# Three empty turns before a node cell's rows, and the first chunk of each unit of layer 3 freed from waiting for the gathering

## The chip, the cores and the metric

The kernel runs on one core of one Trainium2 chip. The metric is device time in microseconds (us) of one execution. A core has a matrix engine (TensorE, in the profile PE, with its weight loads as PEld), a vector engine (VectorE, DVE), an activation engine (ScalarE, ACT), a general engine (GpSimd, POOL) and SyncE (SP), which here only issues transfers (DMAs). Each engine works off its own instructions in a fixed order and waits where an operand isn't ready. Sums of matmuls arise in PSUM, a small memory of eight banks; everything else lies in SBUF or in the chip's main memory.

## What is computed

Four graph layers run over the same 2708 nodes with 256 features and one dense 2708 x 2708 matrix `adj` (non-negative, with a full diagonal). After each layer the input is added and the rows are normalised.

```python
x = _layernorm(x + _L0_gnn_ref(x, adj, ...))   # adj @ (x * W)
x = _layernorm(x + _L1_gnn_ref(x, adj, ...))   # attention with 4 heads
x = _layernorm(x + _L2_gnn_ref(x, adj, adj, ...))
x = _layernorm(x + _L3_gnn_ref(x, adj, ...))
# layer 2, for adj without negative entries
node_support = adj_without_diagonal @ h
edge_output = gru_cell(node_support, h, edge weights)
edge_support = mean over 3 heads of softmax(e_plus where adj > 0) * adj @ (h @ W)
node_output = gru_cell(edge_support, h, node weights)
layer 2 = diag(adj) * edge_output + diag(adj) * node_output
# layer 3
z = concat([x, adj @ (x @ neigh_W.T) / (adj.sum(1) + 1)]) @ lin_W.T
```

## The kernel before

The change touches layers 2 and 3. Both are long products with `adj`, whose columns are cut into three **units** and whose rows into eleven **chunks** of 256. A unit of layer 2 takes 512, 512 and 330 columns from each half of the nodes and goes three times (heads) through the eleven chunks. A unit of layer 3 takes 430, 430 and 366 columns from each half and goes through them once; the last two full tiles of layer 3 are done in another way at the end.

**One chunk** is a call of `seven` (line 299). It makes one step of a fast 2 x 2 block product that needs seven products in place of eight. First DVE forms four sums of the four blocks in `pa` (lines 305 to 308), two of them in a tile `s` that has two buffers. Then PE makes seven products, which the profile shows as fourteen matmuls of line 318. Three of the seven use a block as it was loaded (a11, a12, a22); the other four use a sum. All add up in seven PSUM banks, named m1, m26, m75 and m43. In layer 2, ACT and DVE first make the block from the attention logits (lines 1288, 1291, 1292); in layer 3 the block comes straight from `adj` by SP's transfers (line 265). `pa` has three buffers.

**Gathering.** At the end of a head, or of a unit in layer 3, `gathered` (line 322) reads the seven banks back: a copy by ACT (line 326) and four DVE instructions in the order of lines 329, 332, 335 and 336. The next chunk's products into m26, m75 and m43 have to wait for the reads of these. The last of the four is kept as `summed`.

**Work between the products.** The eighth PSUM bank (`bank`, line 1074, one buffer) serves everything else: projections of a head's result (`project`, line 1115), the gates of the two GRU cells (`cell`, line 1132), the transposes and products of the finished rows (`node_rows` and `rows_end`, lines 1173 and 1184), and layer 3's rows (`rows3`, line 1340). These are Python generators. `between` (line 292) advances the first of them to its next `yield`: this is one **turn**. `urgent` (projections) goes ahead of `later`. `seven` gives a turn after its third and its sixth product, so a chunk has two turns; in the first seven chunks of layer 3's first unit (`early3`, line 1358) there is one after each product. Work that is left is run off without products between, before the first chunk that needs the last rows (line 1361).

`node(u, est)` (line 1226) does the node cell of unit u for its two halves. For one half, `cell` takes eight turns, one for each gate. After the last gate, DVE still has the lines 1165, 1166, 1246 and 1247 to do before the result `yt` is there; this runs in a turn of its own, in which PE gets nothing. Then, in turns of their own, each tile of up to 128 rows is turned (`node_rows`: line 1178, ACT's copy at 1180, moments by DVE and POOL at 171 to 176) and ended (`rows_end`: the product of line 1189, which ACT reads at 1191 and DVE at 1192; then POOL stores the row). The order of turns is rows 0, rows 1, end 0, rows 2, end 1, and so on. Where a tile of rows straddles two units, POOL first copies its part (line 1219). During the first half's rows, the second half's inputs are loaded through POOL's queue (line 1247, issue at line 247), and DVE later mixes them (`prepare`, lines 1240 and 1241).

**Who orders the work.** The program is traced in Python order. The framework then plans each engine's order before the run, by simulated readiness: of the instructions that it takes to be ready, the one that was traced first goes first. An instruction may so stand before one that was traced earlier but is ready later. On the chip this order is fixed. `tc.issue_after(x)` tells the planner to put every instruction of the block that runs on x's engine behind x in that order. In layer 3 it holds the four sums of every chunk behind `summed`, the end of the gathering before:

```python
for i, c in enumerate(lead):
    ...
    with tc.issue_after(summed.ins):
        seven(nright, m, pa, h3, hq[c], c, w, i == 0, i == MH - 1, range(7) if early3 else (2, 5))
y, summed = gathered(nleft, m, w, W, "yk")
```

Of the kernel before, what the change touches and what calls it, by code (L numbers as in the profile page):

```python
# [2 lines left out]

# [24 lines left out]
def kernel(  # L28
# [59 lines left out]
    def sz(i):  # L88
        return min(P, N - i * P)
# [189 lines left out]
    def quarter_sums(pool, b, c, nm):  # L279

        tt = pool.tile([P, 4, P], F32, tag=f"quarter{c}", name=f"{nm}{c}")
        b11, b12 = b[2 * c][:, :P], b[2 * c][:, P:]
        b21, b22 = b[2 * c + 1][:, :P], b[2 * c + 1][:, P:]
        nc.vector.tensor_tensor(tt[:, 0], b12, b11, ALU.subtract)
        nc.vector.tensor_tensor(tt[:, 1], b22, tt[:, 0], ALU.subtract)
        nc.vector.tensor_tensor(tt[:, 2], b12, b22, ALU.subtract)
        nc.vector.tensor_tensor(tt[:, 3], b21, tt[:, 1], ALU.subtract)
        return tt
# [3 lines left out]
    def between():  # L292
        for q in (urgent, later):
            while q:
                if next(q[0], q) is not q:
                    return
                q.pop(0)
# [24 lines left out]
    def gathered(pool, m, w, wide, tag, bufs=1):  # L322

        m1, m26, m75, m43 = m
        m1s = pool.tile([P, wide], F32, tag="m1s", name="m1s", bufs=1)
        nc.scalar.copy(m1s[:, :w], m1[:, :w])
        y = pool.tile([P, FC, 2, wide], F32, tag=tag, name=tag, bufs=bufs)
        yq = y.rearrange("p f h w -> p (f h) w")[:, :, :w]
        nc.vector.tensor_tensor(
            yq[:, 0::3], m1s[:, None, :w].to_broadcast([P, 2, w]), m26[:, :, :w], ALU.add  # L330
        )
        nc.vector.tensor_tensor(
            yq[:, 1:3], yq[:, 3:4].to_broadcast([P, 2, w]), m75[:, :, :w], ALU.add
        )
        nc.vector.tensor_tensor(yq[:, 3], yq[:, 1], m75[:, 1, :w], ALU.add)  # L335
        return y, nc.vector.tensor_tensor(yq[:, 1:3], yq[:, 1:3], m43[:, :, :w], ALU.add)
# [726 lines left out]
    with (  # L1063
# [7 lines left out]
        summed = None  # L1071
# [30 lines left out]
        def accumulators():  # L1102
            return [ps_a.tile([P, W], F32, tag="m1", name="m1")] + [
                ps_a.tile([P, 2, W], F32, tag=nm, name=nm) for nm in ("m26", "m75", "m43")
            ]
# [67 lines left out]
        def node_rows(t, src):  # L1173

            n = sz(t)
            pt = bank()
            for f in range(FC):
                nc.tensor.transpose(pt[:n, f * P : (f + 1) * P], src[:, f, :n], ident)
            y = nleft.tile([P, F], F32, tag="y", name="y", bufs=3)
            nc.scalar.copy(y[:n], pt[:n, :F])  # L1180
            mean, rs = moments(y, n)
            return t, src, y, mean, rs

        def rows_end(t, src, y, mean, rs):

            n = sz(t)
            pz = bank()
            for f in range(FC):
                nc.tensor.matmul(pz[:n], src[:, f, :n], lwn[:, f, :], start=(f == 0), stop=(f == FC - 1))
            nc.vector.tensor_scalar(y[:n], y[:n], mean, rs, ALU.subtract, ALU.mult)  # L1190
            nc.scalar.activation(h3[t][:n], pz[:n, F:], AF.Copy, scale=rs)
            nc.vector.scalar_tensor_tensor(y[:n], pz[:n, :F], rs, y[:n], ALU.mult, ALU.add)
            nc.gpsimd.dma_start(y3_d[t], y[:n])

        def load_cell(lo, w):
            got = []
            for parts, tag in ((xt_d, "xt2"), (edge_d.values(), "et")):
                got.append(nleft.tile([P, FC, W], F32, tag=tag, name=tag))
                load_columns(got[-1], parts, lo, w, nc.gpsimd)
            return got  # L1200

        def load_diag(lo, w):

            dst = nleft.tile([P, W], F32, tag="drow", name="drow")
            src = bass.AP(tensor=diag_d.tensor, offset=diag_d.offset + lo, ap=[[0, P], [1, w]])
            nc.gpsimd.dma_start(dst[:, :w], src)
            return dst

        def by_tiles(lo, w, src, ends, among=range(NT)):

            tiles, at = [], 0
            for t, c0, c1 in pieces(lo, w, among):
                got = src(at, c1 - c0)
                at += c1 - c0
                if c1 - c0 < sz(t):
                    first = t not in ends
                    if first:
                        ends[t] = nleft.tile([P, FC, P], F32, tag=f"yt{len(ends)}", name=f"yt{t}")
                    nc.gpsimd.tensor_copy(ends[t][:, :, c0:c1], got)
                    if first:  # L1220
                        continue
                    got = ends[t]
                tiles.append((t, got))
            return tiles

        def node(u, est):

            a, w = units[u]
            nxt = None
            for h in range(2):  # L1230
                lo = h * NH + a
                xt, et = nxt or load_cell(lo, w)
                drow = load_diag(lo, w)
                yt = nleft.tile([P, FC, W], F32, tag="yt", name="yt")
                parts = [[a[:, j, :w] for j in range(FC)] for a in (xt, et, yt)]

                def prepare(j):

                    xj, ej, _ = (a[j] for a in parts)
                    nc.vector.tensor_tensor(ej, ej, drow[:, :w], ALU.mult)  # L1240
                    nc.vector.tensor_tensor(ej, ej, xj, ALU.add)

                def rest(j):

                    _, ej, yj = (a[j] for a in parts)
                    nc.vector.tensor_tensor(yj, yj, drow[:, :w], ALU.mult)
                    nc.vector.tensor_tensor(yj, yj, ej, ALU.add)

                yield from cell(est[h], xt, yt, w, *node_w, b_node, prepare, rest)
                yield  # L1250
                tiles = by_tiles(lo, w, lambda at, n: yt[:, :, at : at + n], shared)
                got = []
                for i in range(len(tiles) + 1):
                    if i < len(tiles):
                        got.append(node_rows(*tiles[i]))
                        yield
                    if i:
                        rows_end(*got[i - 1])
                        yield
                    if i == 1 and h == 0:  # L1260
                        nxt = load_cell(NH + a, w)
# [15 lines left out]
        for u, (_, w) in enumerate(units):  # L1277
            est = [nleft.tile([P, FC, W], F32, tag="est", name="est", bufs=3) for h in range(2)]
            for k in range(K):
# [23 lines left out]
                y, summed = gathered(nleft, m, w, W, "yk")  # L1303
# [6 lines left out]
        def complete(u):  # L1310

            return [t for t in tiles3 if ends3[t] == u]
# [27 lines left out]
        def rows3(u, y, o8):  # L1340

            a, w = units3[u]
            for h in range(2):
                for t, src in by_tiles(h * NH3 + a, w, lambda at, n: y[:, :, h, at : at + n], shared3, tiles3):
                    pt = room()
                    for f in range(FC):
                        nc.tensor.transpose(pt[: sz(t), f * P : (f + 1) * P], src[:, f, : sz(t)], ident)
                    row3(t, o8[:, complete(u).index(t)], pt)
                    yield
            flush()  # L1350
# [4 lines left out]
        for u, (_, w) in enumerate(units3):  # L1355
            m = accumulators()
            for i, c in enumerate(lead):
                early3 = u == 0 and max(ends_at[2 * c], ends_at[2 * c + 1]) + 1 < len(units)
                if u == 0:
                    if not early3:  # L1360
                        while urgent or later:
                            between()
                    hq[c] = quarter_sums(xqp, h3, c, "hq")
                pa = nright.tile([P, 2, 2, W], F32, tag="p", name="p", bufs=3)
                load_pairs(units3, u, c, pa, NH3, tiles3)
                if i == MH - 3:
                    o8 = hold.tile([P, 4 * W // F, F], F32, tag="blk", name="o8", bufs=2)
                    for j, t in enumerate(complete(u)):
                        nc.gpsimd.dma_start(o8[: sz(t), j], y3_d[t])
                with tc.issue_after(summed.ins):  # L1370
                    seven(nright, m, pa, h3, hq[c], c, w, i == 0, i == MH - 1, range(7) if early3 else (2, 5))
            y, summed = gathered(nleft, m, w, W, "yk")
            later.append(rows3(u, y, o8))
# [287 lines left out]
```

## Time and profile before

| what | value |
|---|---|
| runs before, median (lowest to highest) | 1877.79 us (1877.62 to 1879.04), 3 runs |
| the profiled execution's own time | 1876.67 us |
| its span, first to last instruction | 1874.9 us |
| mean granted clock of TensorE | 0.998 of full speed |
| PE busy | 1833.9 us, 98% of the span |
| DVE busy | 1295.4 us, 69% |
| ACT busy | 691.6 us, 37% |
| POOL busy | 262.0 us, 14% |
| layer 2's heads | first gathering ends at 997.3 us, last at 1625.8 us |
| layer 3's gatherings | lines 329 to 336 at 1730.9, 1788.6 and 1840.2 us |

The span is the time from the first to the last instruction. A row of the timeline gives the start, the length, the engine, the line, the operation, what it writes and reads, how many instructions are merged in it, and in brackets how long the engine was idle before it and what ended that. The list of waits sums such idle times by line and by what ended them. A small letter q after an engine marks its sequencer, which issues transfers. Times of POOL are rough, and a matmul's end is modelled.

### The profile page before, as it was taken

What the parts mean: (1) busy time and instruction counts of PE and PEld (TensorE: products, weight loads), DVE (VectorE), ACT (ScalarE), POOL (GpSimd) and SP (SyncE); (2) the same over time, 40 slices, a digit from 0 to 9 for tenths busy, and PEclk for the clock granted to TensorE, in tenths of its full rate; (3) what the DMA queues carried; (4) which work ended last, traced back from release to release, by engine and by line L of the source; (5) the groups of instructions that cost most, each with busy time, mean ns of one, the idle gap of its engine ahead of it and who ended that gap; (6) DMA issues with size and microseconds to landing.
All of it is one profiled execution on the core that took longest, in us unless ns stands there. A gap on an engine that the chain in (4) does not pass through costs nothing. (4 is left out here: it accounts for less than half of the span.)

```text
span 1874.9 us, 23105 instructions
## 1 busy us (share of the span) xinstructions
PE 1833.9 (98%) x7530; PEld 1033.8 (55%) x7530; DVE 1295.4 (69%) x2302; ACT 691.6 (37%) x1420; POOL 262.0 (14%) x427
## 2 busy tenths in 40 slices
PE   8999999999999999999999999999999999999997
PEld 7788842232345887888444444444445555654555
DVE  5334479999897664754558887777887768855664
ACT  4445410033143203111556665555564555321011
POOL 1211120001012411000002000111100302111111
PEclk9999999999999999999999999999999999999999
DMA  8344410000002667754556665454554535634763
GB/s 296 124 155 146 152 48 1 30 1 11 13 7 69 144 145 186 180 133 114 175 142 204 180 177 155 126 161 124 155 154 110 141 102 132 163 105 116 199 167 117
DMA packets 434653, 237.32 MB, mean 127 GB/s; under 512 B 184299, under 2 KB 421516, under 8 KB 432092
## 3 DMA queue, kind: packets, MB, share of 16 engines
q1 hardware_dynamic: 417438, 207.41, 40.4%
q0 software_dynamic: 8208, 22.59, 3.8%
q10 hardware_dynamic: 8878, 5.76, 1.0%
q8 instruction: 62, 1.02, 0.2%
q14 instruction: 67, 0.55, 0.1%
HBM read 223.00 MB, written 12.66 MB: 126 GB/s over the span
## 5 line engine op out<-in xcount | busy, mean ns | idle before, releaser
L793 DVE SCALAR_TENSOR_TENSOR p<-fall_b,rise,mask 128x1024 f32<-128x1024 f32 (+1 forms) x264 | 293.9, 1157 | 32.5 <-PE den L784 16.7
L1288 ACT ACTIVATE p<-st,e_neg 128x1024 f32<-128x1024 f32 (+1 forms) x198 | 197.3, 1040 | 197.0 <-PE m L318 193.3
L318 PE MATMUL m<-s,xq 128*128 128x512 f32 (+3 forms) x660 | 230.3, 467 | 0.0
L775 PE MATMUL acc<-p,h 128*64 128x512 f32 (+2 forms) x1056 | 214.5, 548 | 0.2 <-ACT sum L806 0.2
L318 PE MATMUL m<-p,xq 128*128 128x512 f32 (+1 forms) x396 | 183.0, 544 | 0.1
L212 PE MATMUL acc<-turn,strip 128*128 128x257 f32 x792 | 181.6, 379 | 0.0
L1291 ACT ACTIVATE p<-p 128x1024 f32<-128x1024 f32 (+1 forms) x198 | 178.7, 942 | 0.2
L305 DVE TENSOR_TENSOR s<-p 128x512 f32<-128x512 f32 (+3 forms) x132 | 81.7, 619 | 125.1 <-PE m L318 96.2
L318 PE MATMUL m<-p,x 128*128 128x512 f32 (+1 forms) x396 | 167.7, 542 | 0.3 <-DVE supt L335 0.3
L318 PEld LDWEIGHTS m<-s,xq 128*128 128x128 f32 x660 | 124.5, 190 | 76.3 <-issue 59.0
L1292 DVE TENSOR_TENSOR p<-p,blk 128x1024 f32<-128x1024 f32 (+1 forms) x132 | 143.0, 1103 | 32.6 <-ACT p L1291 21.9
L212 PEld LDWEIGHTS acc<-turn,strip 128*128 128x128 f32 x792 | 147.3, 190 | 20.3
L775 PEld LDWEIGHTS acc<-p,h 128*64 128x64 f32 x1056 | 69.8, 136 | 138.2 <-issue 128.6
L318 PE MATMUL m<-s,x 128*128 128x512 f32 (+3 forms) x330 | 127.2, 467 | 0.0
L784 PE MATMUL den<-p,h 128*32 128x512 f32 (+2 forms) x1056 | 117.8, 548 | 0.0
L318 PEld LDWEIGHTS m<-p,xq 128*128 128x128 f32 x396 | 74.6, 190 | 76.8 <-issue 61.5
L318 PEld LDWEIGHTS m<-p,x 128*128 128x128 f32 x396 | 74.9, 190 | 75.3 <-issue 61.1
L466 ACT ACTIVATE below<-strip 128x384 bf16<-128x384 f32 x132 | 78.4, 594 | 68.0 <-DMA strip<-in_adj_t_dram 64.5
L306 DVE TENSOR_TENSOR p<-p 128x512 f32<-128x512 f32 (+3 forms) x132 | 82.3, 624 | 1.9
L318 PEld LDWEIGHTS m<-s,x 128*128 128x128 f32 x330 | 62.0, 190 | 39.2 <-issue 35.1
L276 POOL TENSOR_TENSOR blk<-blk,offdiag 128x128 f32<-128x128 f32 (+3 forms) x50 | 30.8, 621 | 371.9 <-DMA blk<-in_adj_t_dram 208.3
L308 DVE TENSOR_TENSOR s<-p,s 128x512 f32<-128x512 f32 (+3 forms) x132 | 81.2, 615 | 2.0
(288 smaller groups left out, 2590.7 us busy)
## 6 DMA issues: line engine op xcount, KB each, us to landing
strip<-in_adj_t_dram SPq DMA_DIRECT2D x19, 1408.0 KB, 6.0
blk<-in_adj_t_dram SPq DMA_DIRECT2D x88, 256.0 KB, 3.4
blk<-in_adj_t_dram SPq DMA_DIRECT2D x88, 192.0 KB, 4.0
pa<-in_adj_t_dram SPq DMA_DIRECT2D x110, 128.0 KB, 2.6
turn<-in_adj_t_dram SPq DMA_DIRECT2D x44, 256.0 KB, 3.2
blk<-in_adj_t_dram SPq DMA_DIRECT2D x88, 128.0 KB, 2.4
p<-in_adj_t_dram SPq DMA_DIRECT2D x88, 128.0 KB, 2.6
turn<-in_adj_t_dram SPq DMA_DIRECT2D x44, 192.0 KB, 3.1
```

Of the source, the lines that this page charges most:

```text
L212: nc.tensor.matmul(acc, s[:, c, :n], rhs(c), start=(c == 0), stop=(c == NT - 1))
L305: nc.vector.tensor_tensor(s1, a21, a22, ALU.add)
L306: nc.vector.tensor_tensor(a21, a21, a11, ALU.subtract)
L308: nc.vector.tensor_tensor(s4, a12, s2, ALU.subtract)
L318: nc.tensor.matmul(dst[:, :w], lt, rt, start=start and not (one_bank and i), stop=stop and not (one_bank and i in (1, 2, 5)))
L466: nc.scalar.activation(below[:, : (hi - lo) * P], s[:, lo:hi].rearrange("p c n -> p (c n)"), AF.Relu, scale=-1.0, accum_out=negative[:, BE ...
L775: nc.tensor.matmul(acc[s][i * HD : (i + 1) * HD, :ws], hs[c][:, 2 * q + i, :HD], ps[i][:, p0 : p0 + ws], **flags,)
L784: nc.tensor.matmul(den[j : j + CT, :ws], hs[c][:, 2 * q + i, HD + 1 - CT :], ps[i][:, p0 : p0 + ws], **flags,)
L793: nc.vector.scalar_tensor_tensor(p[:, :w], falls[g // 2][:, 2 * q + i, :w], rise[:, c, 2 * q + i : 2 * q + i + 1], mask[:, c, at : at + w] ...
L1288: nc.scalar.activation(p[:, :, :w], st_k[:, :, :w], AF.Relu, scale=-1.0, bias=e_neg[:, at, k : k + 1])
L1291: nc.scalar.activation(p[:, :, :w], p[:, :, :w], AF.Exp, scale=-1.0)
L1292: nc.vector.tensor_tensor(p[:, :, :w], p[:, :, :w], blk[:, i, :, :w], ALU.mult)
```

## The change

After the node cell of each half, three `yield`s stand where there was one, so that two more turns pass in which this generator gives PE nothing. And the four sums of the first chunk of each of layer 3's units are no longer held behind `summed`; those of the other ten chunks still are.

```diff
-from contextlib import ExitStack
+from contextlib import ExitStack, nullcontext
...
                 yield from cell(est[h], xt, yt, w, *node_w, b_node, prepare, rest)
-                yield
+                for _ in range(3):
+                    yield
                 tiles = by_tiles(lo, w, lambda at, n: yt[:, :, at : at + n], shared)
...
-                with tc.issue_after(summed.ins):
+                with tc.issue_after(summed.ins) if i else nullcontext():
                     seven(nright, m, pa, h3, hq[c], c, w, i == 0, i == MH - 1, range(7) if early3 else (2, 5))
```

## The prediction

> **What bounds the kernel now.** I read the page's busy line first, then PE's list of waits, then the timeline of PE, DVE and POOL around each wait.
>
> ```profile
> PE 1833.9 (98%) x7530; PEld 1033.8 (55%) x7530; DVE 1295.4 (69%) x2302; ACT 691.6 (37%) x1420; POOL 262.0 (14%) x427
> ```
>
> PE is busy for 98% of the span, and in the timeline matmuls of 512 columns follow each other every 0.43 us. The change takes no matmul away. So all that it can win is time in which PE stands still, and only where the instruction that PE waits for comes earlier. PE's list of waits, its lines for the rows of node cells (L1178) and for layer 3's unit starts:
>
> ```profile
> PE bank L1178 <- DVE y L1192: 5.8, 5, 1.8
> PE m L318 <- DMA p<-in_adj_t_dram: 2.8, 2, 1.4
> PE bank L1178 <- POOL yt L1219: 1.8, 2, 1.6
> PE m L318 <- DVE yk L336: 0.8, 1, 0.8
> PE bank L1347 <- DVE yk L336: 0.4, 1, 0.4
> ```
>
> Total, number, longest. The reader sees the whole stake: 5.8 + 1.8 = 7.6 us at the rows, 2.8 + 0.8 + 0.4 = 4.0 us at unit starts, 11.6 us or 0.6% together.
>
> **The empty turns: where the 7.6 us lie.** There are six node cells (three units, two halves). PE's timeline gives these waits before L1178: first cell none; second 1.83 (at 1320.4); third 1.83 (1480.9) and 0.19 (1487.1); fourth 1.55 (1549.7) and 0.82 (1557.9); fifth 1.15 (1671.0); sixth 0.25 (1701.3). Only the 1.55 and the 0.25 are first rows that wait for the cell's result, by way of POOL's copy. The others are third and fourth rows, which wait for the one bank until L1192 has read it. The third cell, PE and then DVE:
>
> ```profile
> 1478.34 0.72 PE L318 MATMUL m<-p,xq 128*128 128x330 f32 x2
> 1480.88 0.44 PE L1178 MATMUL bank<-ident,yt 128*128 128x128 f32 x2 [1.83 <-DVE y L1192]
> ```
>
> ```profile
> 1478.21 0.69 DVE L1240 TENSOR_TENSOR et<-et,drow 128x512 f32<-128x512 f32 x1 [1.23 <-DMA et<-edget]
> 1478.82 0.41 DVE L1190 TENSOR_SCALAR y<-y,bn_mv,bn_rs 128x256 f32<-128x256 f32 x1
> 1479.14 0.69 DVE L1241 TENSOR_TENSOR et<-et,xt 128x512 f32<-128x512 f32 x1
> 1479.75 0.69 DVE L1240 TENSOR_TENSOR et<-et,drow 128x512 f32<-128x512 f32 x1
> 1480.35 0.48 DVE L1192 SCALAR_TENSOR_TENSOR y<-bank,bn_rs,y 128x256 f32<-128x256 f32 x1
> ```
>
> DVE stood 1.23 us for the other half's input `et`, then mixed it in three instructions of 0.69, all ahead of the L1192 that PE wants: 1.23 + 2.07 = 3.3 us, more than the 1.83. The second cell has the same pattern: 0.83 of waiting at 1311.7 and two L1240 of 0.69 = 2.2 us against 1.83.
>
> Two more turns are one chunk: 14 x 0.43 = 6.0 us at 512 columns, 14 x 0.28 = 3.9 us at 330. The loads of `et` do not move, since they start when L1247 is through with the buffer. So the rows come 6.0 or 3.9 us later and L1240 stays; its wait then falls before the rows, or on row 0 with a turn to spare. I take the 1.83, 1.83 and 0.19 as gone (3.85), bounds 0 and 3.85. In the fourth cell POOL ends its copy at 1549.6, 1.5 us after PE wanted the row; 3.9 us cover that: 1.55 gone. Its 0.82 I leave, since there two L1292 of 0.84 stand ahead of L1192 and every chunk brings two.
>
> The third unit's cells run beside layer 3's first unit, with a turn after each product of 2 x 0.36 us; two turns are 1.4 us. There PE already puts five products between the two halves of the fifth cell's first row, more than three turns ask for, so the plan should hardly change: gain 0, bounds 0 and 1.15 + 0.25.
>
> An empty turn issues nothing, no transfer either, and shortens no queue. Is there room? Units 1 and 2 of layer 2 have 66 turns each for 44 and 46 turns of work (4 + 32 + 8, 4 + 34 + 8); four more fit, and a part of the second node cell slides into the third head. After layer 2, 4 + 32 turns are left for 49 places in the seven early chunks; 4 + 36 fit. If they did not, each would cost its product, 0.7 us, 2.9 for four. POOL's loads for the later half move by two turns with their consumers.
>
> Against this stands that every moved row meets other DVE work. Five such waits now average 5.8 / 5 = 1.16 us; I put one new one of 1.2 against the gain, bounds 0 and 3 x 1.2 (as many as the three that go). Sum of this part: 3.85 + 1.55 - 1.2 = **4.2 us**.
>
> [...] POOL's power (L176) takes 0.54 us at best and 2.06 in the second cell. [...]
>
> **The first chunk's sums: what is late now.** DVE just before layer 3's second unit:
>
> ```profile
> 1724.01 0.61 DVE L308 TENSOR_TENSOR s<-p,s 128x430 f32<-128x430 f32 x1
> 1730.94 1.05 DVE L329 TENSOR_TENSOR yk<-m1s,m 128x860 f32<-128x860 f32 x1 [6.32 <-PE m L318]
> ```
>
> DVE idles 6.32 us, gathers until 1734.87, and only then sums (1734.79 to 1737.88). The first chunk's eight loads are issued from 1721.48 on (the batch before has seven, the first unit's number); the last at 1724.99, and landing takes at most 2.7 us: 1727.7. An `s` buffer is free at about 1727.1, when PE leaves the chunk before the last. Four sums of 0.6 = 2.4 end at 1730.1, 0.8 us ahead of the gathering: hidden in the gap. Third unit: last load 1782.66 + 2.5 = 1785.2, + 4 x 0.55 = 1787.4, against a gathering at 1788.62. So the 0.38 and the 0.80 go; what is late next is L335 at 1791.39, up to 0.4 us after PE could use it, with the next chunk's a11 as filler. Value 1.2, bounds 0 and 1.2.
>
> First unit: loads end issue at 1618.31, landing 3.0 to 3.1 later, 1621.4; sums until 1623.8, while the gathering could start at 1622.58: it is put off by up to 1.2 us. PE here now runs ahead to the next chunks' a11, whose loads are late:
>
> ```profile
> 1626.45 0.96 PE L318 MATMUL m<-p,turn 128*128 128x430 f32 x2 [1.42 <-DMA p<-in_adj_t_dram]
> 1629.52 0.96 PE L318 MATMUL m<-p,turn 128*128 128x430 f32 x2 [1.39 <-DMA p<-in_adj_t_dram]
> ```
>
> With the sums done, PE has the first chunk's ten other matmuls (3.6 us) to do instead. They wait for L329 until 1624.7 in place of 1624.1 and for L335 until 1626.1 in place of 1625.4: some 1.2 us of standing in place of 2.8. If the plan still puts the next chunk's a11 first, the 1.42 stays and the 1.39 goes. Both give about 1.4 to 1.6; I take 1.4, bounds -1.2 (gathering late, nothing won) and 2.8. Sum of this part: 1.4 + 1.2 = **2.6 us**.
>
> **Sum.** 4.2 + 2.6 = 6.8 us. The profiled execution takes 1876.67 (span 1874.9 and 1.8 around it), so 1869.9; the median shown is 1.1 above that execution: 1877.79 - 6.8 = 1871.0 us. 0.2%, about what a measurement of this kernel tells from no change, is 3.8 us.
>
> **Rivals.**
> - *The rows' waits move along.* Two turns are exactly one chunk, so every row meets the same products of DVE in the same places. Then only 1.55 + 2.6 = 4.1 goes: 1873.7. For it: the fourth cell's 0.82, which no load causes. Against it: the two 1.83 have a load's wait in them.
> - *The sums are planned where they were*, because the planner takes the data to come late: 4.2 alone, 1873.6. Against it: DVE's gap of 6.32.
> - *Everything goes*: 11.6, 1866.2.
> - *Slower: the sums hold up the gathering.* DVE takes its order as planned; if the four stand ahead of L329 and their loads come late, L329 waits, and behind it the banks and PE. The batch after the first unit's start took 5.6 to 6.5 us to land in place of 3. With x us more per landing, the gatherings come 1.2 + x, x - 0.8 and x - 1.2 later; this eats the 4.0 at x = 1.6. At x = 3 it costs 8.2 - 4.0 = 4.2 net, 1882.0, if the rows win nothing too.
>
> **Chances.** Forecast 0.50, waits move along 0.24, sums unmoved 0.08, everything 0.10, slower 0.08. The two cases near 4 us lie on the bound of 3.8, half of them on each side: faster 0.76, same 0.16, slower 0.08. The range reaches from everything, 1866, to waits moving along with two new ones, 1873.7 + 2.4, rounded to 1876.5.
>
> **What would show it.** PE's wait for POOL's L1219 falls to 0.3 us or less, that for L1192 to 3 or less; L1240 stands ahead of the rows' L1190. Two or more L305 groups of layer 3 stand before L329, which starts no later than now after PE's last m26. PE's waits for `p`'s loads are halved. It would be wrong if PE waits for L336 or L329 grew, or if new waits of L1178 of over 1 us came at other rows.

## The result and the profile after

| | us | runs |
|---|---|---|
| before, median (lowest to highest) | 1877.39 (1875.71 to 1879.04) | 9 |
| after, median (lowest to highest) | 1883.41 (1878.36 to 1885.66) | 9 |
| after, the profiled execution (its span) | 1883.85 (1882.0) | |

The change makes the kernel slower: the ratio is 1.0025, with a 95% interval from 1.0016 to 1.0035. That is some 5 to 6 us, where 6.8 us of gain were forecast. Four executions in the experiments below were over 50 us slower as a whole; the medians leave them out. The busy line of the page after:

```profile
PE 1838.7 (98%) x7530; PEld 1037.7 (55%) x7530; DVE 1296.1 (69%) x2302; ACT 691.7 (37%) x1420; POOL 260.8 (14%) x427
```

The same number of matmuls keeps PE busy 4.8 us longer. So there is more than waiting in the difference: some matmuls take longer. PE's list of waits after (total, number, longest):

```profile
PE bank L1178 <- DVE y L1192: 10.1, 4, 3.2
...
PE m L318 <- DVE yk L329: 1.8, 1, 1.8
...
PE bank L1178 <- POOL yt L1219: 0.5, 1, 0.5
PE m L318 <- DVE yk L335: 0.3, 1, 0.3
```

POOL's copy (1.8 before) and the unit starts (4.0 before) did fall, to 0.5 and about 2.1, nearly as forecast. But rows now wait 10.1 us for L1192 in place of 5.8: 1.86 us in the second cell, 3.06 in the third, 1.93 in the fourth and 3.24 in the fifth. (In the kernel after, lines behind 1250 stand one higher: L1292 is L1293.) The third cell, PE and then DVE:

```profile
1479.26 0.38 PE L1178 MATMUL bank<-ident,yt 128*128 128x128 f32 x2
...
1481.15 1.88 PE L1189 MATMUL bank<-lwn,yt 128*128 128x512 f32 x4
...
1488.31 0.44 PE L1178 MATMUL bank<-ident,yt 128*128 128x128 f32 x2 [3.06 <-DVE y L1192]
...
1491.13 2.69 PE L1189 MATMUL bank<-lwn,yt 128*128 128x512 f32 x4
```

```profile
1479.86 0.69 DVE L1240 TENSOR_TENSOR et<-et,drow 128x512 f32<-128x512 f32 x1 [2.17 <-DMA et<-edget]
1480.47 0.42 DVE L171 BATCH_NORM_STATS2 bn_st<-y 128x6 f32<-128x256 f32 x1
...
1483.36 0.41 DVE L1190 TENSOR_SCALAR y<-y,bn_mv,bn_rs 128x256 f32<-128x256 f32 x1 [0.46 <-POOL bn_rs L176]
...
1486.24 0.41 DVE L1190 TENSOR_SCALAR y<-y,bn_mv,bn_rs 128x256 f32<-128x256 f32 x1 [0.43 <-POOL bn_rs L176]
1486.57 0.69 DVE L1241 TENSOR_TENSOR et<-et,xt 128x512 f32<-128x512 f32 x1
1487.17 0.69 DVE L1240 TENSOR_TENSOR et<-et,drow 128x512 f32<-128x512 f32 x1
1487.77 0.48 DVE L1192 SCALAR_TENSOR_TENSOR y<-bank,bn_rs,y 128x256 f32<-128x256 f32 x1
```

The rows did come later, and `et`'s load now ends early in them, at 1479.86, in place of behind row 1. But L1240 still stands in DVE's fixed order, now ahead of row 0's *moments* (L171). ACT had copied row 0 by 1478.13; DVE took it up only at 1480.47, because it stood 2.17 us for the load. So row 0's chain came late, row 1's moments and L1190 piled up ahead of row 0's L1192, and so did L1241 and the second L1240. PE ended the product at 1483.0; DVE read it at 1487.77.

The fourth cell's 1.93 is of another kind. There the load's wait of 0.56 is over before the product begins; what stands between the product and L1192 is row 1's moments, a power of 1.84 us on POOL and DVE's products:

```profile
1560.96 0.50 DVE L1240 TENSOR_TENSOR et<-et,drow 128x330 f32<-128x330 f32 x1 [0.56 <-DMA et<-edget]
...
1563.91 1.88 PE L1189 MATMUL bank<-lwn,yt 128*128 128x512 f32 x4
...
1566.04 1.84 POOL L176 TENSOR_TENSOR bn_rs<-bn_rs,neg_half 128x1 f32<-128x1 f32 x1 [1.13 <-DVE bn_rs L175]
...
1569.41 0.48 DVE L1192 SCALAR_TENSOR_TENSOR y<-bank,bn_rs,y 128x256 f32<-128x256 f32 x1
```

The second price is in the lengths of L1189: four matmuls of 512 columns in 1.88 us before the wait, in 2.69 behind it. The view of the same time in windows (time, length, PE's busy time and instructions, granted clock, DMA share, GB/s):

```profile
1480.10:1483.50 3.40, 3.40 (x12) 1.00 0.50 116
1484.90:1488.30 3.40, 0.35 (x2) 1.00 0.51 126
1488.30:1489.40 1.10, 1.09 (x5) 0.97 0.31 70
1489.40:1492.80 3.40, 3.40 (x7) 0.51 0.34 102
1492.80:1496.20 3.40, 3.40 (x14) 1.00 0.75 189
```

1.0 us behind the wait, TensorE is granted half its clock for 3.41 us, and matmuls take about twice their time (two of 330 columns 1.31 us in place of 0.72). That costs 1.7 us more. It happens behind three of the waits (3.06, 1.93 and 3.24 us; the stretch begins 1.0, 1.3 and 1.2 us behind them); nothing like it follows a wait of the rows in the profile of before, whose longest is 1.83.

From 1240 us on, PE's idle gaps over 0.25 us sum to 11.4 us before and 13.0 after. PE is busy for 10.2 us at half clock after, which costs it 5.1 us; before, the clock falls only behind PE's last matmul (at 1866.7 us; the matmul ends at 1862.1). That is 6.7 us, of which matmuls elsewhere, a little closer together, give back some 1.6: from the place where PE's order first differs (1208 us before, 1210 after) to its last matmul PE takes 5.1 us longer. This is close to the difference of the medians. Another 2.2 us of the profiled executions lie ahead of that place, where PE has the same order in both kernels, so they are hardly the change's.

### The profile page after: what moved, and what is told of

Its sections match the earlier page's. It is cut to its first block, busy times and chain, and to the rows that moved or that the text cites. A ratio compares the mean times of both kernels' runs of the same rounds, so it can differ in the third digit from the quotient of the medians.

```text
span 1882.0 us, 23091 instructions
## 1 busy us (share of the span) xinstructions
PE 1838.7 (98%) x7530; PEld 1037.7 (55%) x7530; DVE 1296.1 (69%) x2302; ACT 691.7 (37%) x1420; POOL 260.8 (14%) x427
## 4 chain that ended last, share of the span: by engine, by line
PE 84%; DVE 5%; DMA 5%; issue 2%; ACT 2%; POOL 1%; SPq 1%; ACTq 0%; DVEq 0%; POOLq 0%
PE m L318 38%; PE acc L775 11%; PE acc L212 8%; PE bank L1145 8%; PE den L784 6%; PE gate L1020 4%; PE bank L1121 3%; PE bank L1189 2%; DMA strip<-in_adj_t_dram 1%; PE pm L420 1%; SPq L265 1%; ACT below L466 1%; DMA p<-in_adj_t_dram 1%; PE pq L941 1%; DVE p L1293 1%
## 5 line engine op out<-in xcount | busy, mean ns | idle before, releaser
L1292 ACT ACTIVATE p<-p 128x1024 f32<-128x1024 f32 (+1 forms) x198 | 178.7, 942 | 0.2
L1293 DVE TENSOR_TENSOR p<-p,blk 128x1024 f32<-128x1024 f32 (+1 forms) x132 | 143.1, 1105 | 31.8 <-ACT p L1292 19.9
L1293 DVE TENSOR_TENSOR p<-p,turn 128x1024 f32<-128x1024 f32 (+1 forms) x66 | 71.7, 1104 | 17.9 <-ACT p L1292 15.1
```

Source lines behind the costliest of these rows:

```text
L1292: nc.scalar.activation(p[:, :, :w], p[:, :, :w], AF.Exp, scale=-1.0)
L1293: nc.vector.tensor_tensor(p[:, :, :w], p[:, :, :w], blk[:, i, :, :w], ALU.mult)
```

## The experiments

Two theories stood against each other (a third, C, said that only both parts together cost). **A**: rows wait longer for L1192, and the long ones also halve the clock. **B**: in layer 3's first unit the freed sums hold up the gathering. This is what the trace shows for B, DVE after:

```profile
1628.62 0.61 DVE L305 TENSOR_TENSOR s<-p 128x430 f32<-128x430 f32 x1 [4.92 <-DMA p<-in_adj_t_dram]
...
1630.31 0.84 DVE L329 TENSOR_TENSOR yk<-m1s,m 128x660 f32<-128x660 f32 x1
```

Three of the four sums stand ahead of L329 and wait 4.92 us for their block, and the gathering begins at 1630.31 (1622.6 before). But most of these 7.7 us aren't the sums'. Before, the gathering began 0.27 us after PE took up the product shown here first; in the kernel after, PE takes it up 5.1 us later:

```profile
1622.31 0.72 PE L318 MATMUL m<-p,xq 128*128 128x330 f32 x2
```

```profile
1627.42 0.72 PE L318 MATMUL m<-p,xq 128*128 128x330 f32 x2
```

So the sums hold the gathering up by 2.6 us. All times below are medians; the ratios are to the kernel before, timed on the same chip (medians 1877.27, 1876.35 and 1876.83 in the three groups of four). Between groups a difference of medians can be off by 1 us.

| run | us | ratio (interval) |
|---|---|---|
| turns alone | 1879.41 | 1.0013 (1.0004 to 1.0022) |
| sums alone | 1879.49 | 1.0020 (1.0011 to 1.0029) |
| sums, second and third unit only | 1875.14 | 0.9991 (0.9982 to 1.0000) |
| after, ACT's rows | 1866.47 | 0.9944 (0.9932 to 0.9957) |
| before, ACT's rows | 1867.36 | 0.9946 (0.9932 to 0.9959) |
| before, mixing held | 1876.16 | 0.9992 (0.9983 to 1.0000) |
| after, mixing held | 1870.51 | 0.9961 (0.9948 to 0.9974) |
| before, ACT's rows, sums of late units | 1867.18 | 0.9943 (0.9929 to 0.9957) |
| sums alone, mixing held | 1872.03 | 0.9976 (0.9966 to 0.9986) |
| turns alone, mixing held | 1873.42 | 0.9981 (0.9972 to 0.9990) |
| turns, sums of late units, mixing held | 1871.20 | 0.9970 (0.9960 to 0.9981) |
| eight waits put in | 1920.88 | 1.0241 (1.0222 to 1.0259) |

**The turns alone.**

```diff
-                yield
+                for _ in range(3):
+                    yield
```

> The three empty turns alone; all of layer 3's sums stay behind the gathering. Theory A (the rows' waits are the loss: after the change PE waits 10.1 us for L1192 in place of 5.8, and three of these waits, of 1.9 to 3.2 us, are each followed by about 3.3 us in which matmuls take twice their time, some 1.7 us more each): 5 to 9 us slower than before, since the gain of the sums is missing. Theory B (the early sums hold up the first unit's gathering, which began at 1630.3 in place of 1622.6, and the turns do what was forecast): 2 to 4 us faster than before. Theory C (neither part alone, only both together): within 2 us of before.

2.1 us slower: A's sign, and less than it said. POOL's wait goes (0.2 us), but the rows wait 8.4 us for L1192, 3.7 in the third cell. The fifth cell waits 1.3 us there, not 3.24. So that wait isn't the turns' work.

**The sums alone.**

```diff
-                with tc.issue_after(summed.ins):
+                with tc.issue_after(summed.ins) if i else nullcontext():
```

> The freed sums of the first chunks alone; one empty turn as before. Theory A: 1 to 2.5 us faster than before (PE's waits at the starts of the three units fall from 4.0 to about 2 us in the profile of after), and PE's waits for L1192 stay at about 5.8. Theory B: 4 to 8 us slower than before, with L329 of the last head of layer 2 late by 4 us or more. Theory C: within 2 us of before.

2.2 us slower. A's part of this was wrong, since it took the sums for a gain. But B's reason isn't shown either: at the first unit's start PE waits only 0.7 us, less than before. The loss is in the fifth cell, 45 us later:

```profile
1666.07 0.54 POOL L176 TENSOR_TENSOR bn_rs<-bn_rs,neg_half 128x1 f32<-128x1 f32 x1 [0.66 <-DVE bn_rs L175]
1669.76 0.50 DVE L1240 TENSOR_TENSOR et<-et,drow 128x330 f32<-128x330 f32 x1 [3.84 <-DMA et<-edget]
1670.18 0.41 DVE L1190 TENSOR_SCALAR y<-y,bn_mv,bn_rs 128x256 f32<-128x256 f32 x1
...
1671.33 0.47 DVE L1192 SCALAR_TENSOR_TENSOR y<-bank,bn_rs,y 128x256 f32<-128x256 f32 x1
...
1671.86 0.44 PE L1178 MATMUL bank<-ident,yt 128*128 128x128 f32 x2 [3.77 <-DVE y L1192]
```

Row 1's rs is there at 1666.6. Its L1190 and row 0's L1192 stand behind L1240, which waits 3.84 us for `et`. PE waits 3.77 us and loses 1.7 more at half clock (two matmuls of L1189 then take 1.92 us, where four took 1.88 ahead of the wait); before it waited 1.15. So freeing sums in the first unit has changed DVE's plan at a place that has no sums of a first chunk. As for C: the two parts alone cost 2.1 and 2.2 us, at its bound of 2, and together 4.3 of the 6.0, so most of the loss needs no interplay.

**The sums in the second and third unit only.**

```diff
-                with tc.issue_after(summed.ins):
+                with tc.issue_after(summed.ins) if i or u == 0 else nullcontext():
```

> The freed sums alone, and only in the second and third unit of layer 3; one empty turn as before. Theory A: 0.8 to 1.5 us faster than before, the waits of 0.38 and 0.80 at the two unit starts gone; the first unit's start as before, with two waits of 1.4 for p's loads. Theory B: the same 0.8 to 1.5 faster, and 5 to 9 us faster than the freed sums in all three units.

2.1 us faster, with an interval that reaches no change; forecast were 1.2 for these two units. The fifth cell's wait is 1.5 us. With the sums freed in all units it is 4.4 us slower than this: the loss of this part lies in the first unit, and the traces show it in the fifth cell's rows.

**ACT frees the bank.** The centred unit matrix is added to the weights once; the product then gives the centred row too, and ACT scales both halves.

```diff
...
+                    for f in range(FC):
+                        own = lw[:, f, f * P : (f + 1) * P]
+                        nc.vector.tensor_tensor(own, own, ident, ALU.add)
                     centred(lw[:, :FC])
...
-            nc.vector.tensor_scalar(y[:n], y[:n], mean, rs, ALU.subtract, ALU.mult)
             nc.scalar.activation(h3[t][:n], pz[:n, F:], AF.Copy, scale=rs)
-            nc.vector.scalar_tensor_tensor(y[:n], pz[:n, :F], rs, y[:n], ALU.mult, ALU.add)
+            nc.scalar.activation(y[:n], pz[:n, :F], AF.Copy, scale=rs)
```

> The changed kernel, with the bank of a row's product freed by ACT alone: the centred unit matrix is added to the weights once in layer 0, so that the product holds the centred row too, ACT scales it, and L1190 and L1192 of DVE are gone (two more DVE instructions in layer 0; the same is computed). Theory A: PE's waits for L1192 (10.1 us) and the slow matmuls behind them (about 5 us) go, some 1 to 3 us of other waits come in their place: 9 to 14 us faster than the changed kernel, 3 to 8 faster than before. Theory B: at most the 5.8 us that L1192 cost before go and the first unit's start stays: 4 to 6 us faster than the changed kernel, about as fast as before. If the slow clock doesn't come from these waits, PE's rate after 1480 us stays low in stretches of about 3 us.

> The kernel before, with the bank of a row's product freed by ACT alone (the same edit as in the run on the changed kernel: centred unit matrix in the weights, ACT scales, no L1190 and L1192; the same is computed). The rows' waits of 5.8 us go: 5 to 9 us faster than before. Against the changed kernel with the same edit (1866.47) it tells what the change is worth once no row waits for DVE. If the change's own mechanics are sound (POOL's copy covered 1.55, unit starts 1 to 2.5): this one is 2 to 4 us slower than that. If the first unit's held-up gathering costs by itself: within 1 us of it or faster.

On the changed kernel 1866.47, 17 us faster (15 by the ratios), more than A said; on the kernel before 1867.36. What is left of the changed kernel's waits:

```profile
PE m L318 <- DVE pa L306: 2.5, 4, 1.2
PE m L318 <- DVE yk L329: 2.1, 1, 2.1
```

No row waits for DVE, and from 1240 to 1840 us no stretch at half clock is left: the granted clock is 1.00 in each 60 us of it. With that, the change neither loses nor wins what a measurement can tell: 0.9 us. So the expected 2 to 4 us of gain didn't come, and the 0.9 fell where the expectation had put a cost of the held-up gathering; the runs with the mixing held, below, speak on that. Nor did the late units' sums show their gain here: with ACT's rows they were expected to be 0.8 to 1.5 us faster, and 1867.18 is 0.2 faster than 1867.36. The loss needs DVE's part in the rows (the edit takes two DVE instructions out of each row). These kernels are also the fastest of the study.

**The mixing held behind the rows.** Only DVE's order is constrained: L1240 and L1241 (here 1244 and 1245) come behind the last L1192 (here 1193) that was traced before them.

```diff
...
-                    nc.vector.tensor_tensor(ej, ej, drow[:, :w], ALU.mult)
-                    nc.vector.tensor_tensor(ej, ej, xj, ALU.add)
+                    with tc.issue_after(row_done.ins) if row_done else nullcontext():
+                        nc.vector.tensor_tensor(ej, ej, drow[:, :w], ALU.mult)
+                        nc.vector.tensor_tensor(ej, ej, xj, ALU.add)
...
-                        rows_end(*got[i - 1])
+                        row_done = rows_end(*got[i - 1])
```

> The kernel before, with the mixing of the other half's input (L1240, L1241) held behind the last L1192 of the rows before it in DVE's order; nothing else. Theory A1 (rows wait because L1240 stands ahead of L1192 and waits for et's load): L1192's waits fall from 5.8 to 1.5 to 3.5 us, 2 to 4 us faster. Theory A2 (DVE's plain queue of products, moments and POOL's power is what rows wait for, the load's wait is beside it): L1192's waits stay at 4.5 to 6, within 1.5 us of before.

> The changed kernel with the same hold on the mixing. Theory A1: L1192's waits fall from 10.1 to 2 to 4 us, and with no wait over 1.9 us the stretches of half clock go too: 7 to 11 us faster than the changed kernel, 1 to 5 faster than before. Theory A2: L1192's waits stay at 7 or more, 0 to 3 us faster than the changed kernel. Theory B (gathering of the first unit): as A2.

The changed kernel with it takes 1870.51, 12.9 us less than without (12.0 by the ratios), a little more than A1 said, and 5.8 us less than before. PE's waits there, and its third cell:

```profile
PE bank L1179 <- DVE y L1193: 2.4, 3, 1.5
PE m L318 <- DVE yk L329: 1.7, 1, 1.7
PE bank L1190 <- DVE y L1193: 1.2, 1, 1.2
```

```profile
1476.35 1.88 PE L1190 MATMUL bank<-lwn,yt 128*128 128x512 f32 x4
1480.30 0.44 PE L1179 MATMUL bank<-ident,yt 128*128 128x128 f32 x2
1482.24 1.88 PE L1190 MATMUL bank<-lwn,yt 128*128 128x512 f32 x4
```

The 3.06 us are gone, L1190 keeps its 1.88, and the rows' waits for L1193 are 3.6 us in place of 10.1. No wait of a row leads to half clock (1.00 is granted in each 60 us from 1240 to 1840 us); the fourth cell's wait, 1.48, is the longest of them. This is the main test: no work was taken away, only the place of the mixing. The sums fit: 6.5 us of waits and 5.1 us at half clock are gone, for 12 to 13 us of time.

On the kernel before, the same hold is worth nothing sure, as A2 said, but not for A2's reason. Layer 2's last head is gathered 5.0 us sooner there (1617.6 for 1622.6). Layer 3's first unit gives this back: 112.7 us from that gathering to its own in place of 108.4. Most of it is one row at its end:

```profile
1711.66 0.55 POOL L1383 DMA_DIRECT2D y<-y  x1 [3.08 <-DMA y<-y]
1712.23 0.57 POOL L176 TENSOR_TENSOR bn_rs<-bn_rs,neg_half 20x1 f32<-20x1 f32 x1
...
1714.20 3.41 PE L1190 MATMUL bank<-lwn,yt 128*20 128x512 f32 x4 [2.02 <-DVE y L1193]
```

A load in POOL's queue waits 3.08 us for a row's store, the power stands behind it, DVE behind the power, PE behind DVE: 2.0 us, where nothing waited before, and 1.7 more at half clock (the four matmuls of L1190 take 3.41 us, where four took 1.88 in the row before).

**Each part with the mixing held.**

> The freed sums alone (all three units, one empty turn), with the mixing (L1240, L1241) held behind the rows' last L1192. The freed sums alone cost 2.6 us; their profile has L1240 waiting 3.84 us for et in the fifth cell, and PE 3.77. If that is what they cost (theory A1): no wait for L1192 over 2 us in the fifth cell, 2 to 4 us faster than the freed sums alone, 1 to 3 faster than the kernel before with the same hold (1876.16). If the held-up gathering of the first unit costs by itself (theory B): 2 us or more slower than the kernel before with the same hold.

> The three empty turns alone, with the mixing held behind the rows. The turns alone cost 2.1 us; the turns and the sums with this hold were 5.8 us faster than before. Theory A1: 3 to 5 us faster than before (the forecast's 4.2), L1192's waits 2 to 3.5 us, POOL's L1219 wait of 1.5 gone. If the two parts only work together: within 1.5 us of the kernel before with the same hold (1876.16).

> The changed kernel with the mixing held behind the rows, and the freed sums only in the second and third unit of layer 3. Against the same with the sums freed in all three units (1870.51): theory B, the first unit's sums cost: 1.5 to 4 us faster. If they win what was forecast (1.4, by a shorter wait at the first unit's start: 1.7 in place of 2.8): 0.5 to 1.5 us slower.

Sums alone 1872.03, turns alone 1873.42, both 1870.51, neither 1876.16. So with the mixing out of the way each part wins: the turns 2.7 us, the sums 4.1, both 5.6, each uncertain by some 2 us (by the ratios 2.1, 3.0 and 5.8). The turns alone come as expected, 3.4 us faster than before, but rows still wait 5.3 us for L1193 there, not 2 to 3.5; the sums gain the expected 1 to 3 us over neither or a little more. Theory B had the sums alone 2 us or more slower than neither; they are faster, so B falls. Freeing the first unit's sums too is within the uncertainty (1870.51 against 1871.20), so a cost of the held-up gathering doesn't show.

**Eight waits of known length.** Two small products and a chain of ACT copies between them are put between chunks of layer 3's second and third unit.

```diff
...
+                    with tc.issue_after(last.ins):
+                        g = bank()
+                        one = nc.tensor.matmul(g[:, :P], ident, ident)
+                    nc.scalar.copy(z[:, 0], g[:, :64])
+                    for k in range(steps):
+                        nc.scalar.copy(z[:, (k + 1) % 2], z[:, k % 2])
+                    with tc.issue_after(one.ins):
+                        g = bank()
+                        two = nc.tensor.matmul(g[:, :64], ident, z[:, steps % 2])
+                    held.enter_context(tc.issue_after(two.ins))
...
```

> The kernel before with eight waits put into TensorE's work of layer 3's second and third unit, each between two chunks: a product of 128 columns into the bank, a chain of 4, 7, 10, 13 and 5, 8, 11, 15 copies by ACT, and a product of 64 columns that waits for it; nothing of the result uses them. If a wait of about 1.9 us or more puts TensorE at half its rate for about 3.3 us: no slow matmuls behind the waits below 1.8 us, 1.6 to 1.8 us of lost time behind each above 2.0, whatever its length. If the slow stretches after the rows have another cause (DVE's load, weights, the transposes): none behind these waits, or the loss grows with the length.

Half of this expectation fell. Waits of 1.56, 1.96, 3.67, 2.11, 3.12 and 4.22 us were followed by slow matmuls, 1.5 to 1.7 us of loss each (3.0 behind the 3.12), but 2.84 and another of 3.65 were not. So a wait alone does it, without rows or mixing, yet its length doesn't decide. Its place does. The waits of 1.96, 2.84 and the first 3.67, in windows:

```profile
1757.80:1761.20 3.40, 1.44 (x6) 1.00 0.94 262
1761.20:1764.60 3.40, 3.40 (x7) 0.50 1.04 305
1771.40:1774.90 3.50, 2.16 (x8) 1.00 0.69 176
1774.90:1778.30 3.40, 1.90 (x7) 1.00 0.76 198
1778.30:1781.70 3.40, 3.40 (x11) 1.00 0.01 1
1788.50:1791.90 3.40, 1.01 (x4) 1.00 0.75 197
1791.90:1795.30 3.40, 3.40 (x6) 0.50 0.03 6
```

Behind the 1.96, four matmuls of 430 columns take 3.18 us; behind the 2.84 they take 1.66. The ends of the six slow stretches lie on one grid of 3.413 us, to within 0.01 us; the two of the table begin 30.7 us apart, nine such steps. The profile after has the same step: its three stretches at half clock are each 3.413 us long and begin at 1489.33, 1571.25 and 1677.07 us, 24 and 31 steps apart. The wait of 2.84 falls on an edge of that grid: 1.29 us of idle time in one window and 1.55 in the next, and the clock stays. The wait of 1.96 lies whole in one window, and the next has half clock. I laid such a grid through the six profiles with slow stretches behind 1000 us and summed the idle time in each window: all 15 windows with 1.93 us or more were followed by half clock. Of those with less, up to 1.89, only three were: one of 1.76 in this run, which I can't explain, and two that were themselves in a slow stretch. In the profile after, the windows with 1.93, 2.18 and 2.38 us (the fourth, fifth and third cell's waits) were followed by half clock; the fullest of the others, with 1.86 after and 1.83 before, were not.

## Why the prediction was wrong

- **The failed step** is this one, of the rows: "The loads of `et` do not move ... so the rows come 6.0 or 3.9 us later and L1240 stays; its wait then falls before the rows, or on row 0 with a turn to spare. I take the 1.83, 1.83 and 0.19 as gone (3.85), bounds 0 and 3.85." In the second cell the wait did fall before the rows, and 1.86 us stayed all the same. In the third it fell on row 0, but there was no turn to spare: what stands behind a waiting L1240 on DVE is not row 0's L1192 alone but its moments first, then row 1's, and a second mixing. So the third cell's 1.83 became 3.06. With L1240 put behind the rows, the total comes out as forecast, 1870.51 against 1871.0. That is luck in good part: the turns then win 2.7 where 4.2 were forecast and the sums 4.1 where 2.6 were.
- **The lower bound of 0** left out a loss. The prediction asked how far the rows move away from a wait, not which instructions the planner would put between the wait and them. The planner let L1240 go first as ready; on the chip it still stood 0.6 to 3.3 us for its load in the second to the fifth cell. The fourth cell's 0.82, left as it was, became 1.93 with no load in it; with the turns and the mixing held it is still 1.48, so most of this rise is the turns' own.
- **The price of a wait** was its own length, and "one new one of 1.2". The runs showed a second term: 1.7 us at half clock behind a wait that left PE idle for 1.93 us or more within one window of the grid. Three of these are 5.1 us, more than the whole forecast of the rows (4.2).
- **POOL's copy** (1.55): right, gone with the turns alone. **The third unit's cells** (0 from the turns): right for the turns, where the fifth cell waits 1.3 us for 1.15.
- **The sums, second and third unit** (1.2): right in sign and about in size where tested alone, 2.1 us, though that isn't clear of no change.
- **The sums, first unit** (1.4, bounds -1.2 and 2.8): the start itself went as said, 1.8 to 2.1 us of standing in place of 2.8. The gathering was held up by 2.6 us in the profile after, not 1.2, since the block landed at 1628.6, 8.2 us after the first of its loads was issued (1620.40), where the prediction took 6.1 (1615.29 to 1621.4). No cost of that shows in the runs. What cost was outside the sum: in the new plan DVE comes to L1240 of the fifth cell early and stands there for its load, ahead of L1190 (3.84 us with the sums alone, 3.30 with both parts, 0.27 before).
- **The rivals.** The slower one gave 1882.0, near the result, but by a mechanism that isn't it: the second and third unit's gatherings are no later, 57.4 and 50.2 us after the one before (57.7 and 51.6 before). "The rows' waits move along" fits the second cell alone, which waits 1.86 for 1.83, behind two products of 1.4 and 1.2 us and a power of 1.5, with no load between product and L1192. Even that wait isn't free of the mixing: with it held, 0.34 is left.
- **What was named as a sign of error** came: waits of L1178 over 1 us in four cells, new in the fourth, and a wait of 1.8 us for L329.

## What to carry to other kernels

On an engine that works in a fixed order, an instruction that waits for a load is priced by all that stands behind it, in the new order (with the sums alone, L1240's 3.84 us of waiting cost PE 3.77); shifting its victims by a turn can put it ahead of more of them (the third cell's 1.83 us became 3.06), so hold such work behind them by hand if it isn't urgent. A small change of constraints can move such an instruction somewhere else, 45 us from the edit: read the whole order again. And a wait of PE may be paid twice: those of 1.93, 3.06 and 3.24 us in the profile after cost 1.7 us more each behind them. So cut the longest waits first, not the largest sum.

## What was not expected of the hardware

The granted clock makes the price of a wait a matter of where it falls in a grid: 1.96 us cost 1.7 more and 2.84 cost none in the same execution. Nor does the program set the grid: in the trace's record of the clock the first full clock begins 9.82 us into the span before and 11.36 after, each on the grid of its later changes, although PE has the same order in both up to 1208 us. This fits the spread of the runs, though no trace of the other runs shows it: 7.3 us over the nine runs of the changed kernel, which has four waits of rows near or over 1.93 us, and 1.6 to 3.1 us over five runs each of the kernels with ACT's rows, where no row waits for DVE. The mean granted clock of the nine goes along: 0.998 in the fastest, 0.994 in the three slowest. One stretch of half clock is 0.0009 of the span, so this is some four stretches (an estimate from these numbers; the clock behind the last matmul is in the means too).
